# One band of a depthwise convolution moved from TensorE to VectorE, under a newly computed schedule

## The chip, the cores and the metric

The kernel runs on one core of a Trainium2 chip. The metric is the device time of one execution in microseconds (us). All data are float32.

## What is computed

The reference is one transformer block on images, x of shape (16, 128, 96, 96): an attention over channels with a residual, then a feed-forward part with a 3x3 depthwise convolution and a residual. Cut to what matters:

```python
xn1 = _layernorm(x_hwc, ln1_w, ln1_b)          # over the 128 channels
attn_out = _attention(xn1, wq, wk, wv, wp)     # 8 heads, 16x16 channel attention over all 9216 pixels
x = x + attn_out.transpose(0, 3, 1, 2)
xn2 = _layernorm(x_hwc, ln2_w, ln2_b).transpose(0, 3, 1, 2)
# _ffn, HID = 512:
h1 = einsum('bchw,oc->bohw', xn2, w_in)        # 1x1, 128 -> 512
h2 = conv_general_dilated(h1, w_dw, padding=((1, 1), (1, 1)), feature_group_count=HID)   # 3x3 depthwise
h3 = gelu(h2)
x = x + einsum('bchw,oc->bohw', h3, w_out)     # 1x1, 512 -> 128
```

## The kernel before

**Tiling.** The 16 images are worked on one after another. Each image has 96 rows and is cut into 6 bands of 16 rows, so there are 96 bands (`NG`); a band has 4 units of 4 rows (384 pixels). The 512 hidden channels are 4 chunks of 128. A job is the depthwise convolution of one chunk in one band.

**The path of an image.** The first norm loads x, transposes pixels to partitions on TensorE (L694), takes statistics on VectorE (L701), raises the variance to -1/2 on POOL (L712), scales on ScalarE (L737) and sums a Gram matrix on TensorE (L746). From it `attention` makes one 128x128 matrix, which TensorE applies to all pixels (L643). The second norm does the same as the first without the Gram matrix and puts its result, transposed back (L780, L783), into a ring of rows `xn`. The first norm of the next image runs beside the convolution of the present one.

**The usual job** (`conv_job`). TensorE makes the hidden rows from the ring (L952, 4 or 5 rows a time, into one of 4 PSUM banks), ScalarE evicts them into the chunk's one buffer `h1` (L955), and where the next band needs two of the rows again ScalarE copies them (L947, `halo`). VectorE then makes six of the nine taps, each one instruction over up to 16 x 96 pixels (L982); ScalarE makes products for two taps (L975), and accumulating DMAs issued from POOL add the one product to the other and the sum to the taps (L989). ScalarE ends the job with the GELU (L993), which waits for the last of these DMAs. The very last job of the program has no such DMAs: VectorE makes all eight taps, and the GELU is cut into four units.

**The other path of chunk 3** (`by_matmuls`). In some bands chunk 3 doesn't pass through `h1`: input product and tap are folded into one 128x128 matrix per tap (`comp`), and TensorE makes the convolution as nine matmuls per unit into one PSUM bank (L1047); ScalarE then applies the GELU from PSUM, in three pieces per unit because the left and the right column have a bias of their own (L1062). Which bands do so is set by `by_pe` (L1124): the bands of the first image that `PE_FIRST` lists, 3 of 7 in the images between, and of the last image those whose distance from the last band stands in `PE_LAST` (L24), here 0, 1, 3 and 4, so the last band, the one before it, the third and the second. A band in the usual path takes two halo rows over from the band above it, and hands two down, only if the neighbour's chunk 3 is in the usual path too.

**The output.** `ffn_out` makes, unit by unit, four matmuls (one per chunk, chunk 3 first) into one bank (L1082). For all bands but the last two ScalarE evicts the sum (L1092) and a DMA adds it to the output; for the last two (`LAST_ADDS`) VectorE adds it to the residual in place (L1089), and SP stores it (L1106).

**The order.** All this work is registered with a planner (`Plan`). Each piece has an engine, a cost in ns, a place (a number along the sequence of jobs, plus an offset for its kind from the table `AT`, plus small steps from `STEP`), and the tiles that it reads and writes. `Plan.order` runs through time: whenever an engine is free it takes, of the pieces that are ready and whose buffers are free, the one with the lowest place. The order in which pieces are taken is written out as the program, and each engine runs its own pieces in that order. `SLACK` adds, by engine, to the time at which the plan takes a result for available; `ADD` and `MOVE` are those of the accumulating DMAs and of SP's transfers. Kinds that end in `_0` in `AT` hold for the first image, and for the first two bands of the feed-forward part. The places are scaled by `band` (L1135), the mean number of jobs per band: 341 jobs / 96.

Of the kernel before, what the change touches and what calls it, by code (L numbers as in the profile page):

```python
# [20 lines left out]
RING = 124  # L21
PE_CHUNK = 3
PE_SHARE = [3, 7]
PE_LAST = (0, 1, 3, 4)  # L24
PE_FIRST = [1, 3, 5]
HEAD = 2
LATE1 = 0.0
# [9 lines left out]
LAST_ADDS = 2  # L37
IN_TURN = ("tr", "xb", "x1")
AT = dict(
    load_1=-98.0, load_2=97.25, tables=85.15, weights=-792.45, zeros=79.7, load_a=-138.9, forth_a=-4.35,  # L40
    stats_a=-21.2, variance_a=-32.7, power_a=-106.65, scaled_a=-54.6, gram=7.8, back_a=-40.4, place_a=-40.15,
    attention=-134.7, mix=-2.85, residual=-281.65, mixed=-12.35, add_x=85.8, forth_b=-9.45, stats_b=-42.85,
    variance_b=31.9, power_b=-14.4, shift_b=-138.5, scaled_b=-461.4, back_b=-7.75, place_b=288.55, evicted=90.4,
    add_out=52.9, halo=120.1, hidden=4.7, kept=-885.75, products=643.55, add_last=35.65, tap=248.3,
    add_first=70.15, gelu=273.2, conv=3.75, conv_gelu=-926.85, out=8.15, add=-117.65, store=67.75, mix_0=-49.95,
    residual_0=-107.3, mixed_0=-51.7, add_x_0=25.0, gram_0=363.7, forth_a_0=-122.3, forth_b_0=-8.35,
    stats_a_0=6.3, stats_b_0=31.35, scaled_a_0=-127.55, scaled_b_0=120.9, back_a_0=-24.7, back_b_0=-58.05,
    place_a_0=-41.75, place_b_0=-85.55, shift_b_0=-22.25, late=69.2, store_x2=-58.9, store_x2_0=-116.55,
    variance_a_0=-270.4, variance_b_0=-83.0, power_a_0=-136.0, power_b_0=76.85, attention_0=-297.05,
    load_a_0=-428.55, hidden_0=2.8, kept_0=126.55, products_0=350.15, tap_0=79.7, add_last_0=-519.2,  # L50
    add_first_0=-230.95, gelu_0=18.6, conv_0=2.5, conv_gelu_0=113.55, out_0=6.35, evicted_0=-10.75,
)
STEP = dict(scaled=0.3, hidden=0.1, products=0.5, tap=0.166, conv=1.6, conv_tap=0.03, out=0.8, out_part=0.05)
SLACK = dict(PE=450, DVE=120, ACT=130, POOL=400, ADD=420, MOVE=290)
NORM1_END = 6.0
EARLY = 5
WAIT = dict(POOL=1130, SP=1470, ACT=1470)
# [7 lines left out]
class Plan:  # L65
# [15 lines left out]
    def op(self, engine, ns, place, work, reads, writes, result, own=None, dma=0, two=False):  # L81

        k = len(self.ops)
        needs = {}
        for t in reads:
            if t in self.writer:  # L90
                needs[self.writer[t]] = True
        for t in writes:
            if t in self.writer:
                needs[self.writer[t]] = True
            for r in self.readers.get(t, ()):
                needs[r] = True
        for t in reads:
            self.readers.setdefault(t, []).append(k)
        new = []
        for t in writes:  # L100
            self.writer[t], self.readers[t] = k, []
            if t[0] in self.free and t[:2] not in self.users and t[:2] not in new:
                new.append(t[:2])
        for t in {t[:2]: None for t in (*reads, *writes)}:
            if t[0] in self.free:
                self.users.setdefault(t, []).append(k)
                needs[self.users[t][0]] = True
        needs.pop(k, None)
        self.ops.append((engine, ns, place, work, list(needs), new, result, own or result, dma, two))
# [129 lines left out]
def tile_restormer_block(  # L239
# [166 lines left out]
    def pe(ns, p, f, r, w):  # L406
        op("PE", ns, p, f, r, w, ns + 200 + SLACK["PE"], ns)

    def dve(ns, p, f, r, w, two=False):
        op("DVE", ns, p, f, r, w, ns + 120 + SLACK["DVE"], ns + 125, two=two)  # L410

    def pool(ns, p, f, r, w):
        op("POOL", ns, p, f, r, w, ns + 33 + SLACK["POOL"])

    def add(p, f, r, w, n=BR, dram=False):
        late = T_DRAM if dram else (0, 0.01)
        op("POOL", 800, p, f, r, w, 350 + SLACK["ADD"], late[1], (T_ADD[0] + n * (T_ADD[1] + late[0])) * 108 / 100)

    def move(p, f, r, w, n=XR):
        op("SP", 430, p, f, r, w, 350 + SLACK["MOVE"], dma=n * T_MOVE)  # L420

    def act(ns, p, f, r, w):
        op("ACT", ns, p, f, r, w, ns + 150 + SLACK["ACT"], ns + 144)

# [699 lines left out]
    def by_pe(g):  # L1124
        k = NG - 1 - g
        if g < NB:
            return g in PE_FIRST
        return k in PE_LAST if k < NB else (k + 1) * PE_SHARE[0] // PE_SHARE[1] > k * PE_SHARE[0] // PE_SHARE[1]

# [57 lines left out]
```

## Time and profile before

| | |
|---|---|
| median of 3 runs | 4030.19 us (4029.83 to 4032.23) |
| the profiled execution | 4030.8 us |
| its span, first to last instruction | 4029.1 us |
| granted TensorE clock | 0.999 of full speed |
| busy: PE, DVE, ACT, POOL | 3983.6, 3959.4, 3707.7, 1889.7 us |
| DMA | 832.64 MB, mean 207 GB/s |

PE is TensorE's matmuls, PEld its weight loads (beside the matmuls), DVE is VectorE, ACT is ScalarE. Every float32 matmul stands in the trace as two records, and records of neighbouring instructions overlap, so a count of records is twice that of matmuls, and the pace of a run of equal instructions is read from its length, not from the mean of one record. A line of a timeline gives start, length, engine, source line, operation, the tiles and their shape, the count, and in brackets idle time before it and what ended it. A line of groups gives, after the bar, busy us and mean ns of one, and then the idle time of the engine before these instructions.

### The profile page before, as it was taken

How to read it: one execution, taken by the hardware profiler on the slowest of the kernel's cores; microseconds unless marked ns; L12 is line 12 of the kernel's file. 1: busy time of each engine (PE TensorE's matmuls, PEld its weight loads, DVE VectorE, ACT ScalarE, POOL GpSimd, SP SyncE). 2: the span in 40 equal slices, each digit the busy share in tenths (PEclk: the TensorE clock that was granted, in tenths of full speed). 3: DMA queues.
4: the chain of work that ended last, by engine and by line, in shares of the span. 5: the costliest groups of instructions: out<-in, count | busy, mean ns of one | idle time of the engine just before them, and what ended most of it. 6: DMA issues, size and time to landing. Idle time of an engine off the chain costs nothing. (4 is left out here: it accounts for less than half of the span.)

```text
span 4029.1 us, 51274 instructions
## 1 busy us (share of the span) xinstructions
PE 3983.6 (99%) x17112; PEld 2602.8 (65%) x17112; DVE 3959.4 (98%) x3472; ACT 3707.7 (92%) x7680; POOL 1889.7 (47%) x1594
## 2 busy tenths in 40 slices
PE   9999999999999999999999999999999999999999
PEld 7666666666666666656666666666666666666565
DVE  6999999999999999999999999999999999999998
ACT  7999999899999999989989899999989999999985
POOL 4544455454454544545455453544545544454431
PEclk9999999999999999999999999999999999999999
DMA  5999899999999999999999999999999999999987
GB/s 147 208 197 223 185 214 205 209 225 197 220 222 201 218 203 230 213 202 219 198 216 210 198 220 198 230 205 211 224 194 227 206 217 216 202 221 189 218 177 152
DMA packets 196872, 832.64 MB, mean 207 GB/s; under 512 B 22784, under 2 KB 24320, under 8 KB 196608
## 3 DMA queue, kind: packets, MB, share of 16 engines
q0 software_dynamic: 138672, 677.52, 85.6%
q1 hardware_dynamic: 57936, 151.83, 10.5%
q8 instruction: 137, 2.24, 0.2%
q14 instruction: 127, 1.04, 0.1%
HBM read 150.62 MB, written 149.42 MB: 74 GB/s over the span
## 5 line engine op out<-in xcount | busy, mean ns | idle before, releaser
L982 DVE SCALAR_TENSOR_TENSOR h<-h,ratio,h 128x1520 f32<-128x1520 f32 (+1 forms) x1707 | 2980.5, 1780 | 8.0
L1082 PE MATMUL h<-h,woutT 128*128 128x384 f32 x3072 | 1135.3, 489 | 8.0 <-ACT h L955 7.1
L1047 PE MATMUL h<-xn,comp 128*128 128x380 f32 (+3 forms) x3162 | 1097.7, 476 | 1.8 <-ACT h L955 0.9
L975 ACT ACTIVATE h<-h,ratio 128x1536 f32<-128x1536 f32 (+1 forms) x680 | 1088.7, 1610 | 4.8 <-PE h L1082 2.9
L952 PE MATMUL h<-xn,winT 128*128 128x384 f32 (+3 forms) x2712 | 1059.9, 494 | 5.2 <-ACT h L955 2.2
L989 POOL DMA_DIRECT2D h<-h x680 | 640.2, 968 | 892.2 <-ACT h L975 390.1
L955 ACT ACTIVATE h<-h,beta 128x384 f32<-128x384 f32 (+1 forms) x1314 | 794.1, 632 | 83.0 <-PE h L952 67.6
L1082 PEld LDWEIGHTS h<-h,woutT 128*128 128x128 f32 x3072 | 557.6, 191 | 347.3 <-issue 39.9
L1047 PEld LDWEIGHTS h<-xn,comp 128*128 128x128 f32 x3162 | 567.0, 190 | 312.9 <-issue 16.6
L712 POOL TENSOR_TENSOR rstd_a<-ve_a,mhalf 128x4 f32<-128x4 f32 x288 | 508.8, 1767 | 449.4 <-ACT ve_a L708 429.0
L712 POOL TENSOR_TENSOR rstd_b<-ve_b,mhalf 128x4 f32<-128x4 f32 x288 | 537.1, 1886 | 351.6 <-ACT ve_b L708 337.9
L952 PEld LDWEIGHTS h<-xn,winT 128*128 128x128 f32 x2712 | 485.6, 190 | 276.1 <-issue 21.8
L982 DVE SCALAR_TENSOR_TENSOR h<-h,ratio 128x1536 f32<-128x1536 f32 x341 | 617.7, 1812 | 2.5 <-ACT h L955 1.4
L993 ACT ACTIVATE h<-h 128x1536 f32<-128x1536 f32 (+1 forms) x344 | 520.1, 1514 | 8.4 <-DMA h<-h 4.5
L737 ACT ACTIVATE zT<-pT_b,rstd_b 128x128 f32<-128x128 f32 x1132 | 331.5, 409 | 21.9 <-POOL rstd_b L712 20.7
L737 ACT ACTIVATE zT<-pT_a,rstd_a 128x128 f32<-128x128 f32 x1080 | 318.1, 412 | 3.2 <-POOL rstd_a L712 1.6
L746 PEld LDWEIGHTS g<-zT 128*128 128x128 f32 x2160 | 275.3, 191 | 43.2 <-issue 0.4
L643 PE MATMUL h<-xn,mwT 128*128 128x384 f32 x768 | 296.3, 489 | 3.5 <-ACT h L1062 1.0
L655 POOL DMA_DIRECT2D x<-in_x_dram x189 | 179.2, 964 | 238.4 <-ACT x L652 161.8
L746 PE MATMUL g<-zT 128*128 128x129 f32 x2160 | 285.2, 274 | 0.0
L652 ACT ACTIVATE x<-h,d 128x384 f32<-128x384 f32 x378 | 225.8, 629 | 13.0 <-PE h L643 7.2
L1062 ACT ACTIVATE h<-h,edge 128x376 f32<-128x376 f32 (+2 forms) x558 | 162.6, 387 | 71.2 <-PE h L1047 70.5
(185 smaller groups left out, 3212.6 us busy)
## 6 DMA issues: line engine op xcount, KB each, us to landing
h<-h POOLq DMA_DIRECT2D x567, 768.0 KB, 10.0
h<-h POOLq DMA_DIRECT2D x113, 720.0 KB, 11.9
x<-in_x_dram SPq DMA_DIRECT2D x192, 384.0 KB, 7.8
out_dram<-x SPq DMA_DIRECT2D x190, 384.0 KB, 9.6
x<-in_x_dram POOLq DMA_DIRECT2D x189, 384.0 KB, 10.3
out_dram<-h POOLq DMA_DIRECT2D x94, 768.0 KB, 10.4
out_dram<-x SPq DMA_DIRECT2D x4, 192.0 KB, 1.9
h<-in_L_conv_w_in_dram SPq DMA_DIRECT2D x1, 256.0 KB, 2.8
```

Of the source, the lines that this page charges most:

```text
L643: nc.tensor.matmul(rows(pm), lhsT=mats[i][0], rhs=interior(i, u), start=True, stop=True)
L712: nc.gpsimd.tensor_tensor(rstd, d["ve"], mhalf, ALU.pow)
L737: nc.scalar.activation(zT(q)[:, k, :P], d["pT", q][:, k, :], AF.Copy, scale=d["rstd"][:, t : t + 1])
L746: nc.tensor.matmul(grams[i][:, : P + 1], lhsT=zt[:, :P], rhs=zt, start=(q == 0 and k == 0), stop=(q == NU * TPU // QT - 1 and k == QT - 1),)
L952: nc.tensor.matmul(rows(ph)[:, k : k + m, :], lhsT=winT[:, n, :], rhs=z, start=True, stop=True)
L955: nc.scalar.activation(window(h1_, r, e - r, 1), rows(d.pop(("ph", r))), AF.Identity, bias=beta[:, n : n + 1])
L975: nc.scalar.activation(d["pr", t][:, o0:o1, :], shifted(t, o0, o1), AF.Copy, scale=ratio[:, n, t : t + 1])
L982: nc.vector.scalar_tensor_tensor(h3[:, o0:o1, w0:w1], shifted(t, o0, o1, w0, w1), ratio[:, n, t : t + 1], onto, ALU.mult, ALU.add)
L989: nc.gpsimd.dma_start(out=to[:, o0:o1, :], in_=d["pr", t][:, o0:o1, :], accum_op=ALU.add)
L993: nc.scalar.activation(h3, h3, AF.Gelu)
L1047: nc.tensor.matmul(d["pc"][:, o0 + k : o0 + k + m, w0:w1], lhsT=comp[:, t, :], rhs=z[:, :, w0 + dx : w1 + dx], start=(t == order[0]), stop ...
L1082: nc.tensor.matmul(rows(d["po"]), lhsT=woutT[:, n, :], rhs=h3s[g, n][:, s * UR : (s + 1) * UR, :], start=(k == 0), stop=(k == NCH - 1),)
```

## The change

The second band of the last image is taken out of `PE_LAST`: its chunk 3 goes the usual path (hidden product, taps, products, DMA adds, GELU) in place of 4 x 9 matmuls. There are then 342 jobs. The offsets of the planner (`AT`) are all replaced, and three entries of `SLACK` change, so the order of the whole program is another. Nothing else changes: costs, buffers and the code are the same. Cut to its core:

```diff
-PE_LAST = (0, 1, 3, 4)
+PE_LAST = [0, 1, 3]
...
 AT = dict(
-    load_1=-98.0, load_2=97.25, tables=85.15, weights=-792.45, zeros=79.7, load_a=-138.9, forth_a=-4.35,
+    load_1=-26.6, load_2=-35.1, tables=-1.15, weights=-57.1, zeros=54.55, load_a=-138.4, forth_a=-4.3,
...
-    add_first=70.15, gelu=273.2, conv=3.75, conv_gelu=-926.85, out=8.15, add=-117.65, store=67.75, mix_0=-49.95,
+    add_last=1.45, tap=114.35, add_first=129.85, gelu=260.5, conv=3.75, conv_gelu=-586.1, out=8.15, add=-76.1,
...
-SLACK = dict(PE=450, DVE=120, ACT=130, POOL=400, ADD=420, MOVE=290)
+SLACK = dict(PE=450, DVE=120, ACT=130, POOL=410, ADD=200, MOVE=360)
```

More of the change, by code (lines that the diff above doesn't have):

```diff
@@ L39 @@
 AT = dict(
-    load_1=-98.0, load_2=97.25, tables=85.15, weights=-792.45, zeros=79.7, load_a=-138.9, forth_a=-4.35,
[L41 to L44, printed above, removed]
@@ L45 @@
-    add_first=70.15, gelu=273.2, conv=3.75, conv_gelu=-926.85, out=8.15, add=-117.65, store=67.75, mix_0=-49.95,
[L46 to L49, printed above, removed]
@@ L50 @@
-    load_a_0=-428.55, hidden_0=2.8, kept_0=126.55, products_0=350.15, tap_0=79.7, add_last_0=-519.2,
-    add_first_0=-230.95, gelu_0=18.6, conv_0=2.5, conv_gelu_0=113.55, out_0=6.35, evicted_0=-10.75,
+    load_1=-26.6, load_2=-35.1, tables=-1.15, weights=-57.1, zeros=54.55, load_a=-138.4, forth_a=-4.3,
+    stats_a=-108.2, variance_a=-56.0, power_a=121.85, scaled_a=-147.25, gram=7.75, back_a=-49.05,
+    place_a=-101.15, attention=-134.05, mix=-2.85, residual=-1.05, mixed=-8.2, add_x=322.4, forth_b=-9.4,
@@ new lines @@
+    stats_b=-392.95, variance_b=125.25, power_b=7.8, shift_b=-65.25, scaled_b=-188.15, back_b=-7.95,
+    place_b=432.7, evicted=147.15, add_out=101.65, halo=222.2, hidden=4.7, kept=-523.7, products=787.25,
+    add_last=1.45, tap=114.35, add_first=129.85, gelu=260.5, conv=3.75, conv_gelu=-586.1, out=8.15, add=-76.1,
+    store=18.5, mix_0=-315.4, residual_0=432.85, mixed_0=-63.05, add_x_0=4.55, gram_0=-5.3, forth_a_0=-41.9,
+    forth_b_0=-8.55, stats_a_0=-27.0, stats_b_0=8.5, scaled_a_0=-384.85, scaled_b_0=188.3, back_a_0=-5.0,
@@ L52 @@
+    back_b_0=-35.3, place_a_0=127.65, place_b_0=-16.0, shift_b_0=-104.65, late=322.55, store_x2=-133.3,
+    store_x2_0=134.5, variance_a_0=-34.45, variance_b_0=-95.6, power_a_0=-49.25, power_b_0=12.65,
+    attention_0=-318.85, load_a_0=-402.4, hidden_0=3.1, kept_0=-35.65, products_0=322.35, tap_0=11.0,
+    add_last_0=26.85, add_first_0=101.1, gelu_0=-0.75, conv_0=2.6, conv_gelu_0=85.7, out_0=6.45,
+    evicted_0=-0.95,
 )
 STEP = dict(scaled=0.3, hidden=0.1, products=0.5, tap=0.166, conv=1.6, conv_tap=0.03, out=0.8, out_part=0.05)
-SLACK = dict(PE=450, DVE=120, ACT=130, POOL=400, ADD=420, MOVE=290)
+SLACK = dict(PE=450, DVE=120, ACT=130, POOL=410, ADD=200, MOVE=360)
```

## The prediction

> **What bounds the kernel now.** I read the page first, then stages, then the last microseconds engine by engine. The first line of the page and its clock row:
>
> ```profile
> PE 3983.6 (99%) x17112; PEld 2602.8 (65%) x17112; DVE 3959.4 (98%) x3472; ACT 3707.7 (92%) x7680; POOL 1889.7 (47%) x1594
> PEclk9999999999999999999999999999999999999999
> ```
>
> Two engines are full, TensorE and VectorE; the clock is not the issue. A share over the whole span cannot say which of the two decides, so I cut the span into start, middle, last stage and tail (columns: window, length, then busy us of PE, PEld, DVE, ACT and POOL):
>
> ```profile
> 0.00:100.00 100.00, 90.99 (x556) 71.19 (x557) 65.70 (x158) 73.14 (x214) 47.29 (x79) 1.00 0.55 146
> 100.00:3790.00 3690.00, 3657.09 (x15767) 2389.88 (x15766) 3668.31 (x3161) 3460.65 (x7165) 1780.19 (x1457) 1.00 0.98 210
> 3790.00:4012.40 222.40, 222.40 (x753) 134.26 (x753) 221.54 (x148) 170.81 (x298) 62.21 (x60) 1.00 0.90 179
> 4012.40:4029.10 16.70, 13.13 (x41) 7.41 (x39) 3.82 (x8) 3.14 (x5) 0.00 (x0) 0.96 0.25 95
> ```
>
> VectorE is idle for 34.3 us of the first 100 (100 - 65.70), for 21.7 us of the next 3690, for 0.9 us of the 222.4 after that, and then its stream of taps is over. So the time at which its last tap ends is its work plus some 57 us of idleness, nearly all of it far from the last image. TensorE has no gap at all between 3790 and 4012.4. The two timelines of the end show who finishes last (start, length, engine, line):
>
> ```profile
> 4002.02 5.45 PE L1047 MATMUL h<-xn,comp 128*128 128x384 f32 x18
> 4007.31 18.22 PE L1082 MATMUL h<-h,woutT 128*128 128x384 f32 x56
> ```
>
> ```profile
> 4004.99 0.56 DVE L1089 TENSOR_TENSOR x<-h,x 128x384 f32<-128x384 f32 x1
> 4005.45 7.05 DVE L982 SCALAR_TENSOR_TENSOR h<-h,ratio,h 128x1425 f32<-128x1425 f32 x4
> 4012.42 1.01 DVE L1089 TENSOR_TENSOR x<-h,x 128x384 f32<-128x384 f32 x2
> ...
> 4025.57 0.56 DVE L1089 TENSOR_TENSOR x<-h,x 128x384 f32<-128x384 f32 x1 [2.02 <-PE h L1082]
> ```
>
> The last tap ends at 4012.4. At that moment TensorE is in the middle of an unbroken run of 28 matmuls (two records each) of the output projection, which lasts to 4025.5; seven units of it were still to do when it began, three of them of the band before the last. In the waits of VectorE the same thing stands as one row:
>
> ```profile
> DVE x L1089 <- PE h L1082: 9.9, 5, 2.1
> ```
>
> So the kernel ends TensorE-bound: VectorE is through early, and five residual adds wait for matmuls that are late because TensorE is behind.
>
> **What the change moves.** Chunk 3 of the second band of the last image goes from nine matmuls per unit on TensorE to the path that all other jobs take: hidden product, six VectorE taps, two products by ScalarE that DMAs add. The chain of waits, in order of time, has one unit of either kind of matmul by itself (start, length, records):
>
> ```profile
> 3991.26 5.76 PE h L1047 x18
> 3997.02 5.16 PE h L1082 x16
> ```
>
> *TensorE.* A unit costs 5.76 us, the four units of the band 23.04. What comes instead is the hidden product of 16 rows, four matmuls over 384 columns; by the second row one takes 5.16 / 8 = 0.645 us, so 2.58. TensorE sheds 20.5 us. From 3790 on it had 222.4 + 13.1 = 235.5 us of work without a gap; now 215.0, so it could be through at about 4005.
>
> *VectorE.* It gains six taps. Seven taps of the stage before the end:
>
> ```profile
> 3920.96 1.81 DVE L982 SCALAR_TENSOR_TENSOR h<-h,ratio 128x1536 f32<-128x1536 f32 x1
> 3922.69 10.36 DVE L982 SCALAR_TENSOR_TENSOR h<-h,ratio,h 128x1520 f32<-128x1520 f32 x6
> 3932.96 1.81 DVE L982 SCALAR_TENSOR_TENSOR h<-h,ratio 128x1536 f32<-128x1536 f32 x1
> ```
>
> From 3920.96 to 3932.96 are 12.00 us for seven, 1.714 each (the records overlap, so the mean of one record is too long). Six are 10.3 us. Nothing hides them: between 3790 and 4012.4 VectorE has 0.9 us of room, and before that it is full too. With an equal amount of idleness the last tap ends at 4012.4 + 10.3 = 4022.7.
>
> *ScalarE, DMA, POOL.* Forms of the last image (busy us of the group, mean ns):
>
> ```profile
> L975 ACT ACTIVATE h<-h,ratio 128x1536 f32<-128x1536 f32 x44 | 69.9, 1598 | 0.3
> L993 ACT ACTIVATE h<-h 128x1536 f32<-128x1536 f32 x30 | 45.4, 1513 | 0.6 <-DMA h<-h 0.5
> L955 ACT ACTIVATE h<-h,beta 128x384 f32<-128x384 f32 x75 | 43.4, 597 | 5.5 <-PE h L952 5.3
> L1062 ACT ACTIVATE h<-h,edge 128x376 f32<-128x376 f32 x18 | 10.5, 584 | 22.0 <-PE h L1047 21.9
> L1062 ACT ACTIVATE h<-h,edge 128x4 f32<-128x4 f32 x36 | 7.7, 276 | 0.0
> L947 ACT COPY h<-h 128x192 f32<-128x192 f32 x20 | 7.3, 365 | 0.0
> L993 ACT ACTIVATE h<-h 128x384 f32<-128x384 f32 x4 | 1.9, 512 | 3.7 <-DVE h L982 3.7
> ```
>
> Added: two products 3.20, one GELU 1.51, four evictions 2.39, and one halo copy 0.37, since band 0 now hands two rows on: 7.5 us. Removed: per unit a GELU of 376 columns and two of 4, 0.58 + 2 x 0.28 = 1.14, so 4.5. ScalarE pays 3 us net in a stage where it is idle for 51.6 (222.4 - 170.8); I take nothing, and 3 us if that cover were gone. The two accumulating DMAs of 768 KB are issued from POOL, idle for most of that stage, and land about 10 us later:
>
> ```profile
> h<-h POOLq DMA_DIRECT2D x567, 768.0 KB, 10.0
> ```
>
> That latency stands between the last tap of a job and its GELU, but the added job lies in the second of six bands, so it delays nobody at the end. The DMA share of the last stage is 0.90 against 0.98 before, room for 22 us of transfers (a tenth of 222.4). Nothing again, bounded by one late landing, 10 us, if the job were the last.
>
> *The tail.* With TensorE through early, three of four partial products of each of the last four units can lie ready in the four PSUM banks before the last tap. After it there remain: four GELUs of one unit each, 1.9 us (last row of the ScalarE fence), one matmul 0.65, one add 0.56, and from the end of the last add (4026.13) to the end of the span 2.97: 6.1, and some 0.4 for hand-overs, so 6.5 for the 16.7 of before. The adds of the band before the last may now lie ahead of the last tap: three more than before at 0.5 each (two in 1.01), up to 1.5. The end is then 4022.7 + 6.5 = 4029.2 to 4030.7; I take 4030.0, against a span of 4029.1. The profiled execution took 4030.8, 1.7 above its span and 0.6 above the median of the runs, so 4030.0 becomes 4031.7 and on the scale of the median 4031.
>
> Put in one line: 9 to 10 us won in the tail, 10.3 lost in the VectorE stream.
>
> *The schedule computed anew* cannot be read from the trace, only bounded. It moves no work, but it redraws all idle time of VectorE. Of 15 consecutive windows of 250 us, the fullest and the emptiest:
>
> ```profile
> 350.00:600.00 250.00, 246.59 (x1080) 162.50 (x1079) 246.54 (x214) 230.73 (x482) 117.57 (x99) 1.00 0.95 204
> 2850.00:3100.00 250.00, 247.78 (x1061) 161.02 (x1060) 249.54 (x215) 233.77 (x485) 128.74 (x101) 1.00 1.00 214
> ```
>
> Idle 3.46 and 0.46 us; the mean over the 3690 us is 21.7 / 14.8 = 1.47. All windows like the best would give 15 us, all like the worst would cost 30. The start, with its 34.3, may give or take a third, 11. As the old schedule shows both kinds of window, I take no shift, and 7 us to either side as what one redraw usually does: 4024 to 4038.
>
> **The rivals.**
>
> *The tail keeps its length* (slower). If the partial products are not made ahead, TensorE does all four of a unit after that unit's GELU: 0.5 + 4 x 2.58 + 0.56 + 2.97 = 14.4, so the time is 4022.7 + 14.4 + 1.1 = 4038; at 16.7 as now, 4040.5. It decides from the point at which fewer than three quarters of the last band's output matmuls lie before the last tap. For it: all 16 matmuls of the last band come after 4012.4 now. Against it: they were late because TensorE was behind, and 17.7 us of that are gone (4022.7 - 4005). The Trainium skill, "Perfetto Trace Analysis", section "Identifying the Most-Contended Engine", speaks for this side: matmul busy time misjudges TensorE, which is to be judged by its weight loads, while occupancy is fair for VectorE. By that rule TensorE, at 65%, has room, VectorE at 98% is the bound alone, and the change would pay its 10.3 us in full, 4040.5. This trace disagrees for the last stage: the weight loads fill 60% of it (134.26 of 222.40), yet 28 matmuls in 18.22 us are 0.65 each, their bare pace.
>
> *The new order feeds VectorE worse* (slower). A shorter allowance for the DMA adds (ADD 420 to 200) lets the plan put a GELU ahead of its data, and ScalarE works in order; evictions behind it come late, then taps. Idle windows of 2.7 us in place of 1.47 would give 18 us, so 4049. For it: ScalarE already waits thus, if seldom. Against it: only three times in 4029 us:
>
> ```profile
> ACT h L993 <- DMA h<-h: 4.5, 3, 2.4
> ```
>
> *The new order feeds it better* (faster). Two thirds of the best case in the middle, 10, and 8 of the start: 4013. For it: the 34.3 us at the start are long. Against it: the change sheds TensorE work only in the last image, where VectorE has no idle time to win back.
>
> *TensorE decides alone* (faster): 4030 - 20.5 = 4010. The chain of waits, nearly all PE, speaks for it; the VectorE stream, which must then end 10 us earlier than its work allows, against it.
>
> **How the numbers follow.** Swap even, 4024 to 4038: 0.46. Tail kept, 4038 to 4041: 0.13. Fed worse, 4040 to 4055: 0.20. Fed better, 4008 to 4022: 0.18. TensorE alone: 0.03. A measurement of this kernel tells about 0.2%, 8 us, from no change, so faster is below 4022 and slower above 4038: faster 0.21, same 0.46, slower 0.33. The range 4016 to 4047 leaves out TensorE alone, half of fed better and a third of fed worse, together 0.19.
>
> **What would show it.** Right: 72 records of conv matmuls fewer in the last image (four units of 18), the last tap ending near 4023, gaps of some 18 us in all on TensorE after 3790, and a last run of output matmuls that is broken by waits for the GELU of single units and ends within 4 us of the last tap. Wrong: VectorE's idle time outside the tail other than 57 us by more than 7; a last tap before 4016 or after 4030; or a closing run of 16 matmuls behind the last tap.

## The result, and the profile after

The changed kernel took 4023.94 us (median of 20 runs, 4020.96 to 4033.94), the kernel before, on the same chip, 4031.73 (20 runs, 4028.59 to 4046.83). The ratio is 0.9981, 95% interval 0.9975 to 0.9988: some 8 us faster, at the edge of what I had called no change, and on the other side of the forecast (0.8 us slower).

The execution of the changed kernel that was profiled first took 4033.94 us, 10 us above its median, for a reason that is shown below. A second profile of the same program (`again`, 4022.0 us) is near the median, and it stands here for the profile after. Its first line and its stages:

```profile
PE 3968.7 (99%) x17048; PEld 2591.3 (64%) x17048; DVE 3963.6 (99%) x3478; ACT 3707.7 (92%) x7676; POOL 1924.0 (48%) x1596
```

```profile
0.00:100.00 100.00, 90.34 (x554) 70.06 (x555) 66.69 (x155) 73.76 (x209) 42.67 (x77) 1.00 0.58 148
100.00:3790.00 3690.00, 3664.14 (x15801) 2394.42 (x15800) 3673.84 (x3175) 3463.66 (x7185) 1819.01 (x1462) 1.00 0.99 211
3790.00:4012.40 222.40, 209.90 (x684) 124.56 (x683) 220.82 (x147) 169.53 (x283) 62.36 (x59) 0.96 0.88 176
4012.40:4020.30 7.90, 4.33 (x14) 2.26 (x12) 2.23 (x4) 0.74 (x2) 0.00 (x0) 1.00 0.28 100
```

VectorE has six instructions more (3478 for 3472), TensorE 64 records fewer (72 of the convolution less 8 of the hidden product). The busy share of VectorE rises from 98% to 99%: its idle time between 100 and 3790 us falls from 21.7 to 16.2. The end, TensorE and VectorE:

```profile
3993.02 5.45 PE L1048 MATMUL h<-xn,comp 128*128 128x384 f32 x18
3998.31 18.42 PE L1083 MATMUL h<-h,woutT 128*128 128x384 f32 x56
```

```profile
4009.64 1.71 DVE L983 SCALAR_TENSOR_TENSOR h<-h,ratio,h 128x1440 f32<-128x1440 f32 x1
4012.90 1.85 DVE L1090 TENSOR_TENSOR x<-h,x 128x384 f32<-128x384 f32 x3 [1.56 <-PE h L1083]
4016.77 0.56 DVE L1090 TENSOR_TENSOR x<-h,x 128x384 f32<-128x384 f32 x1 [2.02 <-PE h L1083]
```

The last tap ends at 4011.3 (before 4012.5), and the span 9.0 us later (before 16.6). The last band's units now come in a group of three and a single one, so nearly all its partial products were ready. Still, TensorE's closing run of 28 matmuls is unbroken, as before (18.42 us, before 18.22).

The span fell by 8.8 us, and four terms make it up. VectorE's busy time up to its last tap went from 3955.7 to 3961.4 (+5.7), its idle time from 56.9 to 49.9 (-7.0: -1.0 in the first 100 us, -5.7 from 100 to 3700, -0.3 after), the tail from 16.6 to 9.0 (-7.6). The six taps at 1.714 are 10.3, so the other instructions of VectorE must have become 4.6 us cheaper.

Laying the program's list of taps beside the start times shows where. A tap that follows a tap of another job starts 128 ns plus 1.04 ns per element after it. A tap that follows one of its own job, and so reads what that one wrote, starts 118 ns later still, in the mean of the 224 such pairs in the profile before; the least of them is 102 ns late, while only 11 of 1222 pairs of different jobs are more than 30 ns late. Of the 118 ns, 36 stand as idle time between the two records and 82 within the busy time: two independent taps overlap in the record by some 80 ns, and a tap that waits gives up this overlap first. The timelines show it without the list. The last four taps of before, all of the last job and of 1425, 1425, 1536 and 1440 elements, take 4012.42 - 4005.45 = 6.97 us, where the rule for independent taps gives 6.58: 0.39 for three pairs. Four taps of 1425 and 1520 elements that alternate between two jobs, in the profile after, take 3990.89 - 3984.24 = 6.65, just what the rule gives:

```profile
3984.24 6.73 DVE L983 SCALAR_TENSOR_TENSOR h<-h,ratio,h 128x1425 f32<-128x1425 f32 x4
3990.89 1.80 DVE L983 SCALAR_TENSOR_TENSOR h<-h,ratio 128x1536 f32<-128x1536 f32 x1
```

The changed kernel has 183 such pairs, 41 fewer. Their hidden part is 3.4 of the 4.6 us, and their visible part, 1.5 us, is among the 7.0 us of idle time. Of the 1.2 us that remain, about 1.0 is the same overlap given up by statistics that start late behind a tap, 19 in place of 31.

**Why the first profile was 10 us longer.** Some powers on POOL (L713) took four to six times as long as the median. The rows are min/median/max ns, first of `after`, then of `again`:

```profile
L713 POOL TENSOR_TENSOR rstd_a<-ve_a,mhalf x288: 997/1824/10582, 6.3 to 3693.1; 128x4 f32<-128x4 f32 x144
```

```profile
L713 POOL TENSOR_TENSOR rstd_a<-ve_a,mhalf x288: 997/1820/3893, 6.7 to 3687.8; 128x4 f32<-128x4 f32 x144
```

In `after` one of three long ones ran from 3705.20 to 3714.13. ScalarE waited for it, and VectorE, which had ended its last tap at 3713.24, stood still until the attention step behind it:

```profile
3705.20 8.93 POOL L713 TENSOR_TENSOR rstd_b<-ve_b,mhalf 128x4 f32<-128x4 f32 x1 [0.55 <-ACT ve_b L709]
```

```profile
3714.16 1.14 ACT L738 ACTIVATE zT<-pT_b,rstd_b 128x128 f32<-128x128 f32 x4 [4.94 <-POOL rstd_b L713]
```

```profile
3717.50 0.28 DVE L848 TENSOR_TENSOR wide<-g,ncq 1x128 f32<-1x128 f32 x1 [4.27 <-issue]
```

The two executions are the same program: last tap at 4023.3 and 4011.3, tail 9.0 in both.

### The profile page after: what moved, and what is told of

It reads as the page before. It is cut to its first block, busy times and chain, and to the rows that moved or that the text cites. A ratio compares the mean times of both kernels' runs of the same rounds, so it can differ in the third digit from the quotient of the medians.

```text
span 4032.2 us, 51195 instructions
## 1 busy us (share of the span) xinstructions
PE 3973.7 (99%) x17048; PEld 2593.8 (64%) x17048; DVE 3964.5 (98%) x3478; ACT 3704.6 (92%) x7676; POOL 1939.2 (48%) x1596
## 3 DMA queue, kind: packets, MB, share of 16 engines
q1 hardware_dynamic: 57936, 151.83, 10.4%
q14 instruction: 127, 1.04, 0.1%
## 4 chain that ended last, share of the span: by engine, by line
PE 75%; DVE 11%; ACT 8%; DMA 2%; issue 2%; POOL 2%; POOLq 0%; DVEq 0%; ACTq 0%; SPq 0%
PE h L1083 19%; PE h L1048 19%; PE h L953 16%; DVE h L983 10%; PE g L747 6%; PE h L644 4%; PE pB_a L781 3%; PE pT_a L695 3%; PE pB_b L781 2%; PE pT_b L695 2%; ACT h L976 2%; ACT h L956 1%; POOL rstd_b L713 1%; ACT zT L738 1%; DMA x<-in_x_dram 1%
## 5 line engine op out<-in xcount | busy, mean ns | idle before, releaser
L1048 PE MATMUL h<-xn,comp 128*128 128x380 f32 (+5 forms) x3090 | 1074.7, 478 | 4.4 <-ACT h L956 3.7
L990 POOL DMA_DIRECT2D h<-h x682 | 628.7, 957 | 885.2 <-ACT h L976 399.5
L1048 PEld LDWEIGHTS h<-xn,comp 128*128 128x128 f32 x3090 | 557.2, 191 | 312.5 <-issue 22.2
L713 POOL TENSOR_TENSOR rstd_a<-ve_a,mhalf 128x4 f32<-128x4 f32 x288 | 527.5, 1844 | 447.1 <-ACT ve_a L709 428.0
L713 POOL TENSOR_TENSOR rstd_b<-ve_b,mhalf 128x4 f32<-128x4 f32 x288 | 564.6, 1986 | 351.4 <-ACT ve_b L709 346.2
L781 PEld LDWEIGHTS pB_b<-ident,zT 128*128 128x128 f32 x1152 | 147.0, 142 | 111.0 <-issue 52.2
## 6 DMA issues: line engine op xcount, KB each, us to landing
out_dram<-h POOLq DMA_DIRECT2D x94, 768.0 KB, 10.3
```

The lines of the kernel that those rows point to most:

```text
L713: nc.gpsimd.tensor_tensor(rstd, d["ve"], mhalf, ALU.pow)
L990: nc.gpsimd.dma_start(out=to[:, o0:o1, :], in_=d["pr", t][:, o0:o1, :], accum_op=ALU.add)
L1048: nc.tensor.matmul(d["pc"][:, o0 + k : o0 + k + m, w0:w1], lhsT=comp[:, t, :], rhs=z[:, :, w0 + dx : w1 + dx], start=(t == order[0]), stop ...
```

## The experiments

Sixteen runs: fourteen edited kernels, and the changed kernel itself twice (`again`, `control`). All ratios are to the kernel before on the same chip; its median was 4033 to 4042 us in these batches, so results are compared by ratio and not in us. The table gives what the profile of each shows; idle and busy are VectorE's up to the end of the last tap, pairs are successive taps of one job, long powers are those over 4 us.

| kernel | ratio (95%) | last tap | tail | idle 0-100, 100-3700, rest | busy | pairs | long powers |
|---|---|---|---|---|---|---|---|
| before | 1 | 4012.5 | 16.6 | 34.3, 21.5, 1.1 | 3955.7 | 224 | 0 |
| again | 0.9971 (0.9959 to 0.9984) | 4011.3 | 9.0 | 33.3, 15.8, 0.8 | 3961.4 | 183 | 0 |
| band_only | 1.0008 (0.9999 to 1.0017) | 4025.4 | 10.3 | 33.8, 25.5, 1.8 | 3964.3 | 191 | 1 |
| sched_only | 1.0014 (1.0005 to 1.0024) | 4025.8 | 18.0 | 34.1, 33.6, 1.8 | 3956.4 | 230 | 2 |
| two_less | 1.0050 (1.0038 to 1.0063) | 4029.9 | 20.9 | 34.3, 22.1, 3.5 | 3970.0 | 175 | 3 |
| pin_band | 1.0007 (0.9994 to 1.0020) | 4032.7 | 8.2 | 34.3, 32.8, 0.3 | 3965.3 | 204 | 4 |
| pin_sched | 0.9973 (0.9962 to 0.9984) | 4012.8 | 16.6 | 34.7, 23.0, 2.3 | 3952.8 | 201 | 2 |
| scale_before | 0.9999 (0.9990 to 1.0008) | 4017.8 | 18.1 | 34.0, 26.3, 2.1 | 3955.2 | 217 | 1 |
| scale_after | 1.0009 (1.0000 to 1.0018) | 4030.0 | 8.6 | 33.1, 31.3, 0.3 | 3965.3 | 202 | 2 |
| pairs_after | 1.0040 (1.0028 to 1.0052) | 4042.9 | 13.7 | 35.7, 43.7, 2.0 | 3961.5 | 97 | 3 |
| pairs_before | 1.0034 (1.0021 to 1.0047) | 4040.3 | 16.6 | 33.1, 51.7, 3.6 | 3951.9 | 122 | 6 |
| pin_two | 1.0019 (1.0009 to 1.0029) | 4033.4 | 19.4 | 33.2, 21.6, 7.3 | 3971.2 | 187 | 3 |
| slack_old | 1.0021 (1.0011 to 1.0031) | 4037.2 | 12.8 | 35.5, 34.2, 4.6 | 3962.9 | 168 | 2 |
| control | 0.9980 (0.9969 to 0.9992) | 4014.5 | 9.0 | 33.2, 18.4, 1.4 | 3961.4 | 183 | 1 |
| move_014 | 0.9972 (0.9963 to 0.9981) | 4022.5 | 8.3 | 35.7, 18.1, 6.4 | 3962.3 | 185 | 2 |
| move_012 | 1.0015 (1.0003 to 1.0028) | 4027.8 | 19.4 | 33.1, 20.5, 11.0 | 3963.2 | 200 | 3 |
| last1 | 0.9999 (0.9988 to 1.0010) | 4016.7 | 14.5 | 34.6, 15.9, 5.7 | 3960.5 | 191 | 0 |

A profile is one execution, and with long powers it can lie 10 us above the median of its kernel; the ratios are the verdicts, the columns say where the time is.

**again** (no edit).

> The changed kernel once more, for a second profile: the first one took 10 us longer than the median of its runs. In it three powers on POOL (L713) took 7.9, 10.6 and 8.9 us where the median is 1.9, and the last of them held VectorE up for 4.3 us. Theory (the long powers are an accident of that execution): this execution has none above 4 us, takes 4020 to 4025 us, VectorE's last tap ends at 4013 to 4016 and the tail behind it is 6.5 to 9 us. Rival (they belong to the new order, and the median has them too): powers of 8 us stand at the same three places, the last tap ends at 4013 or earlier and the rest is tail.

Median 4022.38. No power above 3.9 us, last tap at 4011.3: 2 us earlier than expected, the tail as expected. The long powers come in some executions of a program and not in others.

**band_only**

```diff
-PE_LAST = (0, 1, 3, 4)
+PE_LAST = [0, 1, 3]
```

> The kernel before with PE_LAST = [0, 1, 3] alone; offsets and slack of before. Theory (the swap is even, the gain lies in the new order): within 4 us of before, since 9 to 10 us of tail are exchanged for 10.3 us of taps. Rival (the band is the gain, VectorE takes the taps into idle time or contention that it sheds): 6 to 10 us faster than before.

1.0008: the rival falls, the band without the new offsets wins nothing.

**sched_only**

```diff
-PE_LAST = [0, 1, 3]
+PE_LAST = [0, 1, 3, 4]
```

> The changed kernel with the second band of the last image back on TensorE (PE_LAST 0, 1, 3, 4); offsets and slack of after. Theory (the gain lies in the new order): 6 to 10 us faster than before, like the changed kernel itself. Rival (the band is the gain): within 3 us of before, with an unbroken TensorE run that ends 13 us or more behind the last tap.

1.0014: my theory falls in this form too. Each half alone loses, and the two together win. Either they need each other, or the edit did more than it says: it changes the number of jobs, so `band`, by which all places are scaled, and with it the order from the first image on. The table points to the second: idle time from 100 to 3700 us, where no image has the changed band, went from 15.8 to 33.6, more than its two long powers explain (three in `after` cost 12 us).

**two_less**

```diff
-PE_LAST = [0, 1, 3]
+PE_LAST = [0, 3]
```

> The changed kernel with one more band of the last image off TensorE (PE_LAST 0 and 3). Theory (after the change VectorE sets the end): one band more costs 6 taps of 1.714 us, 10.3 us, with at most 2 us of tail left to win, so 8 to 10 us slower than the changed kernel. Rival (TensorE still sets the end): 3 us or more faster than the changed kernel.

TensorE does not set the end, but 1.0050 is three times the loss that I expected from taps. The end of its TensorE timeline shows a wait that neither theory had:

```profile
4016.83 4.34 PE L1083 MATMUL h<-h,woutT 128*128 128x384 f32 x8 [6.79 <-ACT h L994]
4028.83 18.06 PE L1083 MATMUL h<-h,woutT 128*128 128x384 f32 x48 [7.67 <-ACT h L994]
```

With chunk 3 of the last band but one in the usual path, its output matmuls wait twice for a GELU that waits for its DMA adds, and 24 matmuls of 18 us stand behind it.

So the next runs held the scale fixed: all engines' orders are then the same as in the kernel that is edited, up to the band in the last image.

**pin_band** (edit to before)

```diff
-PE_LAST = (0, 1, 3, 4)
+PE_LAST = [0, 1, 3]
...
-    band = len(jobs) / NG
+    band = 341 / NG
```

> The kernel before with PE_LAST = [0, 1, 3], its own offsets and slack, and the scale of places pinned to the old 341 / 96, so that every engine's order is that of before up to the second band of the last image. This is the band alone, without another order. Theory (the swap by itself is about even; the gain is the order of the other 15 images): six taps of 1.714 us less 20 pairs of taps of one job that follow each other (82 ns each) put the last tap 8.7 us later, 4021; the tail falls from 16.6 to 9 or 10 us; so 4029 to 4033 us, from 1 us faster to 2 us slower than before. Rival (the band is the gain): 6 to 9 us faster than before.

**pin_sched** (edit to after)

```diff
-PE_LAST = [0, 1, 3]
+PE_LAST = [0, 1, 3, 4]
...
-    band = len(jobs) / NG
+    band = 342 / NG
```

> The changed kernel with the second band of the last image back on TensorE, and the scale pinned to 342 / 96, so that every engine's order is that of after up to that band. This is the new order without the band. Theory (the gain is the order): last tap 8.7 us earlier than in the changed kernel, 4002 to 4003; tail 16 to 18 us; so 4019 to 4023 us, within 2 us of the changed kernel and 8 to 13 us faster than before. Rival (the band is the gain): 4029 us or more.

This pair settles the cause. The band under the old order: 1.0007 (0.9994 to 1.0020). The new order without the band: 0.9973 (0.9962 to 0.9984), as fast as with it (`again` 0.9971, `control` 0.9980). The fastest executions say the same: 4030.0 us for `pin_band`, 4020.4 for `pin_sched`, and 4030.1 for the kernel before on that chip. The exchange at the end happens about as it was costed. Closing run, last tap and last add of `pin_band`:

```profile
4019.06 18.22 PE L1082 MATMUL h<-h,woutT 128*128 128x384 f32 x56
```

```profile
4029.09 3.56 DVE L982 SCALAR_TENSOR_TENSOR h<-h,ratio,h 128x1536 f32<-128x1536 f32 x2
...
4037.32 0.56 DVE L1089 TENSOR_TENSOR x<-h,x 128x384 f32<-128x384 f32 x1 [0.73 <-PE h L1082]
```

and of `pin_sched`:

```profile
4007.63 18.22 PE L1083 MATMUL h<-h,woutT 128*128 128x384 f32 x56
```

```profile
4011.08 1.71 DVE L983 SCALAR_TENSOR_TENSOR h<-h,ratio,h 128x1440 f32<-128x1440 f32 x1
...
4025.89 0.56 DVE L1090 TENSOR_TENSOR x<-h,x 128x384 f32<-128x384 f32 x1 [2.02 <-PE h L1083]
```

With three bands VectorE's last tap ends 13.6 us behind the start of the closing run, with four 5.2; the tail is 8.2 in the one and 16.6 in the other. The last tap itself is late in both profiles, by long powers (16.4 us in `pin_band`, 7.9 and 7.4 in `pin_sched`), so my expected 4021 and 4002 can't be read off them. VectorE's busy time can: 9.6 us more in `pin_band` than in before, 8.6 less in `pin_sched` than in `again`.

**scale_before** and **scale_after**

```diff
-    band = len(jobs) / NG
+    band = 342 / NG     # scale_before; 341 / NG in scale_after
```

> The kernel before, its own four bands, offsets and slack, but places scaled by 342 / 96 jobs per band in place of 341 / 96, which redraws the order of all engines from the first image on. Theory (a set of offsets fits only the scale for which it was found; the losses of band_only and sched_only came from this, not from the band): VectorE idles 3 to 12 us more between 100 and 3790 us, 3 to 12 us slower than before. Rival (any redraw is as good): within 3 us of before.

> The changed kernel, its own three bands, offsets and slack, but places scaled by 341 / 96. Theory (offsets fit only their scale): VectorE idles 3 to 12 us more between 100 and 3790 us, and 19 more pairs of taps of one job cost 1.6 us; 5 to 14 us slower than the changed kernel, so that nothing or less than nothing is left of its gain. Rival (any redraw is as good): within 3 us of the changed kernel.

By the ratio the redraw of before is as good as before, 0.9999, and my theory misses. But its idle time from 100 to 3700 us is 4.8 us longer (one long power is in it), and its fastest execution, 4033.8 us, is 3.8 slower than the fastest of before on that chip, 4030.1, both within what I had expected; the ratio hides it, since before varied up to 4046.2 there and this kernel to 4041.8. The redraw of after loses all of the gain, 1.0009. VectorE's column from 100 to 3700 us (the third busy number) shows how, in before, again, scale_before and scale_after:

```profile
100.00:3700.00 3600.00, 3570.49 (x15424) 2336.12 (x15423) 3578.52 (x3083) 3374.70 (x6997) 1740.59 (x1420) 1.00 0.98 211
```

```profile
100.00:3700.00 3600.00, 3577.88 (x15471) 2342.01 (x15470) 3584.16 (x3096) 3382.86 (x7026) 1775.63 (x1427) 1.00 0.99 211
```

```profile
100.00:3700.00 3600.00, 3569.55 (x15412) 2338.51 (x15411) 3573.65 (x3081) 3368.66 (x6993) 1778.80 (x1419) 1.00 0.98 210
```

```profile
100.00:3700.00 3600.00, 3565.04 (x15391) 2331.96 (x15391) 3568.68 (x3081) 3358.94 (x6987) 1755.34 (x1419) 1.00 0.98 210
```

Idle 21.5, 15.8, 26.3 and 31.3 us. So a change of 0.3% in the scale destroys the gain of the new order, and costs the old one little or nothing.

These two also make pairs with the first two experiments: up to the band in the last image `band_only` has the order of `scale_before`, and `sched_only` that of `scale_after`. With and without the band the ratios are 1.0008 and 0.9999, 1.0009 and 1.0014. So under four orders the band by itself is worth 0.1% or less either way, with intervals of about that width.

**pairs_after** and **pairs_before**

```diff
-        op("DVE", ns, p, f, r, w, ns + 120 + SLACK["DVE"], ns + 125, two=two)
+        op("DVE", ns, p, f, r, w, ns + 120 + SLACK["DVE"], ns + 400, two=two)
```

> The changed kernel, but the plan takes a VectorE result to be ready for the next VectorE instruction 400 ns after the first ends in place of 125. The work is the same; the new order has 97 pairs of taps of one job in direct succession in place of 183. Theory (each such pair costs 82 ns, whatever stands around it): VectorE's busy time up to the last tap falls by 86 x 82 ns = 7.1 us against the changed kernel's 3961.4, to 3954 or 3955; the time falls by as much only if the redraw costs no idleness, so 4015 to 4035 us. Rival (the 82 ns are a matter of what POOL or the DMAs do beside it): busy time as before, 3960 or more.

> The kernel before with the same edit: 122 such pairs in place of 224. Theory: busy time up to the last tap falls by 102 x 82 ns = 8.4 us from 3955.7 to 3947 or 3948; idle time redrawn, between 100 and 3700 us 15 to 35 us; 4018 to 4036 us. Rival: busy time 3954 or more.

Both theories fall in part. Each pair that is left still costs 118 ns in the mean, 82 of them hidden, 97 of 97 and 122 of 122. But the busy time fell by nothing and by 3.8 us, not by 7.1 and 8.4: in `pairs_after` more statistics (L702) wait behind a tap, 77 of 513 in place of 19 of 516, and the first 80 ns of each such wait are hidden in the overlap of records as those of a pair are. The rest of these waits is part of the 28 and 30 us of idle time that the redraws cost. The price of a pair is firm; that an order with fewer pairs is faster by their sum is not shown.

**pin_two** (edit to after)

```diff
-PE_LAST = [0, 1, 3]
+PE_LAST = [0, 3]
...
-    band = len(jobs) / NG
+    band = 342 / NG
```

> The changed kernel with PE_LAST = [0, 3], the scale of places pinned to 342 / 96, so that every order is that of the changed kernel up to the band before the last. Theory (VectorE's price of a band is six taps, and the 32 us that two_less lost were 10 us of taps, a redraw and a GELU of the second last band that waits for its DMA adds at the head of the queue): last tap 9 to 11 us later than in the changed kernel, 4020 to 4022; TensorE idles behind that GELU; tail 9 to 18 us; 4031 to 4041 us. Rival (TensorE sets the end): faster than the changed kernel.

Busy time up to the last tap rises by 9.8 us, as expected; the tail is 19.4, somewhat over the range. 9.8 + 10.4 = 20 us over `again`, and the ratios differ by 0.0048, 19 us. The last tap is later than expected by long powers (three, as in the first profile of after). The same GELU waits as in `two_less` stand in its TensorE timeline; by subtraction the other 12 us of `two_less` (1.0050 against 1.0019) are its redrawn order.

**slack_old** (edit to after)

```diff
-SLACK = dict(PE=450, DVE=120, ACT=130, POOL=410, ADD=200, MOVE=360)
+SLACK = dict(PE=450, DVE=120, ACT=130, POOL=400, ADD=420, MOVE=290)
```

> The changed kernel, its offsets and its three bands, with the old SLACK (POOL 400, ADD 420, MOVE 290). Theory (offsets, slack and scale were found together and the gain is theirs jointly): a redraw that loses the gain, 4029 to 4043 us, by idle time of VectorE of 20 to 33 us between 100 and 3700 us in place of 15.8. Rival (the offsets alone carry the gain): within 3 us of the changed kernel.

1.0021, idle 34.2 us from 100 to 3700: the offsets alone don't carry the gain; offsets, slack and scale do so together.

**control** (no edit), **move_014**, **move_012** (scale pinned to 342 / 96)

```diff
-PE_LAST = [0, 1, 3]
+PE_LAST = [0, 1, 4]     # move_014; [0, 1, 2] in move_012
```

> The changed kernel once more, as the measure for the three others on the same chip. Both theories: 0.2 to 0.3% faster than before; tail 9 us.

> PE_LAST = [0, 1, 4] in place of [0, 1, 3], scale pinned: the same three bands' worth of matmuls, but one of them a band earlier (the second band of the last image, not the third). Order as in the changed kernel up to there. Theory (TensorE still sets the tail, since its relief came too early in the image and went into waits): the closing run of 28 output matmuls starts about 2 us earlier, last tap as before, tail 6.5 to 7.5, 1.5 to 2.5 us faster than the control. Rival (VectorE sets the end, the tail is its handover): within 1 us of the control.

> PE_LAST = [0, 1, 2], scale pinned: the matmuls of one band come a band later (the fourth band, not the third), nearer to the end. Theory (TensorE sets the tail): TensorE's work lies later, the closing run ends later, tail 11 us or more, 2 to 10 us slower than the control; 1.4 us of that by 17 more pairs of taps of one job. Rival (VectorE sets the end): 0 to 2 us slower.

Moving a TensorE band earlier shortens the tail by 0.7 us, not by 2, and the intervals of the two overlap (0.9963 to 0.9981 and 0.9969 to 0.9992): no difference shown. Moving it later brings TensorE back as the bound: the closing run starts only 2.4 us before the last tap ends, and the tail is 19.4.

```profile
4025.35 18.22 PE L1083 MATMUL h<-h,woutT 128*128 128x384 f32 x56
```

So in the changed kernel both engines end about together; TensorE decides the last 2 to 3 us (9.0 us of tail against the 6.5 for a TensorE that is through early).

**last1** (edit to after)

```diff
-LAST_ADDS = 2
+LAST_ADDS = 1
```

> LAST_ADDS = 1: the four residual adds of the second last band leave VectorE; ScalarE evicts and a DMA adds to the output, as for all earlier bands. Order as in the changed kernel up to the last image. Theory (TensorE sets the tail): the last tap comes 2 us earlier (four adds at 0.5), but TensorE's closing run stays, so the tail grows by as much and the time is within 1.5 us of the control. Rival (VectorE sets the end): 2 us faster.

0.9999, 0.2% slower than the control; both theories fall. TensorE comes to the end late: its closing run starts at 4009.39, in the control at 4001.43, while the last tap is only 2.2 us later. The run itself has no gap, so ScalarE's copies don't hold it up; TensorE lost its time earlier, most of it in waits for evictions of hidden rows in the last image (first row below, after 3700 us, where the control has 2.1 us). Why these came late was not found.

```profile
PE h L1048 <- ACT h L956: 9.4, 2, 6.3
4009.39 18.22 PE L1083 MATMUL h<-h,woutT 128*128 128x384 f32 x56
```

No version beat the changed kernel beyond the intervals; `pin_sched` and `move_014` equal it.

## Why the prediction was wrong, step by step

Two steps failed. The one that turned the sign is that the new order was put at nothing; a smaller one, the other way, is the size of the tail. The last tap, forecast at 4022.7, ended at 4011.3, before the 4016 that I had named as a sign of being wrong.

**The bound of before: right.** VectorE full with some 57 us of idle time, the end set by a late TensorE. Making TensorE later still (`move_012`) gives that picture again.

**The price on VectorE: right but for the pairs.** Six taps were 10.3 us. The band also brought 20 pairs fewer (224 to 204 under the pinned order), 2.4 us at 118 ns that I didn't count.

**The tail: right in kind, mis-sized.** I said 6.5; it is 9.0, a gain of 7.6 and not of 10. What failed here is "it could be through at about 4005": TensorE ended its run at 4016.7. The 20.5 us were shed, but TensorE waited 12.5 us between 3790 and 4012.4 (222.4 - 209.9), where it had not waited at all. The two largest causes in its waits after 3790 (us in total, times, longest):

```profile
PE pB_b L781 <- ACT xn L784: 4.9, 3, 2.3
PE pT_b L695 <- DMA x<-in_x_dram: 3.2, 2, 2.6
```

And the waits cost more than their length. The clock in that stage's row is 0.96, where before had 1.00: behind TensorE waits of 2.1 to 2.6 us stand three stretches at half clock, in `again` (window, length, busy us of PE, PEld, DVE, ACT and POOL, clock):

```profile
3823.80:3827.20 3.40, 3.04 (x9) 2.35 (x10) 3.40 (x3) 3.26 (x8) 0.00 (x0) 0.51 1.06 184
3844.30:3851.10 6.80, 4.69 (x10) 2.65 (x10) 6.80 (x7) 5.50 (x9) 2.21 (x3) 0.50 1.05 213
3885.30:3892.10 6.80, 5.97 (x13) 3.56 (x14) 6.80 (x5) 5.78 (x10) 0.92 (x1) 0.50 1.04 212
```

There a record of 384 columns takes 0.64 us in place of 0.32, so of the 13.7 us of TensorE's work in these stretches about half, 7 us by estimate, is lost. As TensorE had also done 7 us more before 3790 (3664.14 against 3657.09), 4005 + 12.5 + 7 - 7 gives 4017.5, near the measured 4016.7. The closing run was not broken by waits for single GELUs, as I had forecast, but late.

**The swap: right that it is even, by terms that are each off.** The forecast was 10.3 lost and 9 to 10 won. The terms measured are 10.3 - 2.4 - 7.6 = 0.3 us slower: errors of some 2 us on either side cancel, which is luck. `pin_band` has 1.0007 (0.9994 to 1.0020), and `pin_sched` and the changed kernel are equal.

**The new order: the step that failed.** "I take no shift" for the redraw, 7 us to either side. It was worth 0.27% alone (`pin_sched`, interval 0.16% to 0.38%), 11 us. The terms, from `again` against before, give 9.2: 6.3 of idle time (7.0 less 0.7 for the band's 20 pairs), 1.7 for the hidden part of the other 21 pairs and 1.2 of other hidden waits. `pin_sched`'s own profile shows only the 2.9 of busy time, 3952.8 against 3955.7; its idle time is longer than that of before, but this execution has two long powers and took 4031.2 us, 5.5 above its median. I had bounded the idle time at -15 to +30 in the middle and had not looked for hidden time inside the busy time at all. The rival "fed better" named the mechanism and its two places, but both too large: 10 for 5.7 in the middle, 8 for 1.0 at the start. Part of it is visible in VectorE's waits for transposes, 3.0 us less in `again`; what the rest of the idle time comes from was not traced. Before, then again:

```profile
DVE st_b L701 <- PE pT_b L694: 6.1, 12, 1.2
```

```profile
DVE st_b L702 <- PE pT_b L695: 3.1, 7, 1.1
```

My reason against that rival, that the change sheds TensorE work only in the last image, spoke of the band and not of the schedule. I found nothing in the trace of before that tells a good order from a bad one. Of the redraws made here (band_only, sched_only, scale_before, scale_after, slack_old, two_less and the two pairs kernels) none had less idle time from 100 to 3700 us than the old order, and only the change itself did. That its offsets, slack and scale fit each other, where the redraws changed one of them alone, is the likely reason; it is argued, not shown.

**"Fed worse", by ADD 420 to 200.** The waits did come, 4.5 us of GELUs behind DMA adds before, 20.9 in `again`. They cost nothing that the trace shows: all eight lie between 3925 and 4008 us, where neither TensorE nor VectorE has a gap.

```profile
ACT h L994 <- DMA h<-h: 20.9, 8, 7.7
```

**"The tail keeps its length"** would have had 4038 or 4040.5; the tail fell by 7.6. The rule beside it, of the Trainium skill, "Perfetto Trace Analysis", section "Identifying the Most-Contended Engine", would have had 4040.5 too. That TensorE at 64% weight loads can be full is confirmed by the closing run of `again`: 28 matmuls in 18.42 us, 0.66 each.

## What to carry to other kernels

When a change moves work and redraws an order, run the two apart, and hold everything fixed that the edit changes by the way; here the number of jobs scaled all places, and the first two undo experiments measured that and not their edit. On an engine that is full, look for time inside its busy share: start-to-start distances of equal instructions, sorted by what stands before them, found 26 us in 224 dependent pairs, 18 of which no idle column shows. Work taken off one engine comes back as a gain only as far as the order lets that engine run ahead; the rest turns into waits, and on TensorE, here, into stretches at half clock behind them.

## What the runs showed of the hardware

**A VectorE tap right behind the tap that it depends on costs 118 ns more** than one behind an independent tap (medians of 1.83 against 1.71 us from start to start for 1520 elements), in every pair counted. Only 36 ns of that stand as idle time.

**TensorE waits of 2 us and more can be followed by a half clock.** In `again` every stretch at half clock after 3790 us, 3.4 or 6.8 us long, stands behind such a wait. In before and `pin_sched`, where TensorE has no wait above 0.5 us from there to the last tap, there is none. Not every such wait has one: in before nothing follows the wait of 2.6 us at 542 us. What decides it was not measured.

**A POOL power can be shut out by a chain of VectorE taps.** While it waits, VectorE runs without a gap. In `pin_band`, POOL, then VectorE:

```profile
1450.43 16.40 POOL L712 TENSOR_TENSOR rstd_a<-ve_a,mhalf 128x4 f32<-128x4 f32 x1
```

```profile
1452.12 1.83 DVE L982 SCALAR_TENSOR_TENSOR h<-h,ratio 128x1536 f32<-128x1536 f32 x1
1453.85 12.09 DVE L982 SCALAR_TENSOR_TENSOR h<-h,ratio,h 128x1520 f32<-128x1520 f32 x7
1465.84 0.77 DVE L701 BATCH_NORM_STATS2 st_b<-pT_b 128x6 f32<-128x256 f32 x2
```

The power ended once VectorE had come to the statistics; the one at 3705 us ended 0.9 us after VectorE's last tap, when there was nothing left to run. Usually a power gets in at the next boundary between two taps: in the profile before 412 of the 432 boundaries at which one waited. But it can miss several, and then often at the same places: under the new order at 171, 305 and 3705 us (`after`, `control`, `pin_two`, `move_014`, `move_012`, `pin_sched`), each time for about the same 6.7, 7.9 and 8.9 us, and not in every execution. Others came once only, as those of 10.6 us in `after` and 7.4 in `pin_sched`. By the last taps of single executions one such miss cost 3 us (`control` against `again`), three cost 12. The Trainium skill, "SBUF — State Buffer", section "SBUF: two separate sides", says that the two engines share a pair of ports as an exclusive lock, held for a whole instruction, and that a VectorE instruction with two SBUF inputs takes it against a GpSimd instruction that reads SBUF. The trace agrees as to whole instructions, a median of 1.8 us where the shortest power took 1.0. That a power can be passed over at eight boundaries in a row, as in this fence, goes beyond it. What decides whether it is passed over was not found.
